# Row differences and sums of the first convolution's bands made on GpSimd during attention

## The chip, the cores and the metric

The kernel runs on one core of a Trainium2 chip. The metric is the device time of one execution in microseconds (us); the median of three executions of the kernel before is 2505.46 us.

## The reference, cut to what matters

The input `x` is 4 images of 128 channels and 64 x 64 pixels in float32. Two layers follow each other:

```python
# layer 0: attention over all 4096 pixels of an image, 4 heads of 32 channels
x_norm = group_norm(x)
q, k, v = split(einsum('oc,bchw->bohw', qkv_w, x_norm) + qkv_b, 3)
attn = softmax(einsum('bhid,bhjd->bhij', q, k) * d ** -0.5)
y0 = x + einsum('oc,bchw->bohw', proj_w, einsum('bhij,bhjd->bhid', attn, v)) + proj_b

# layer 1: two 3x3 convolutions with weights quantized to 3 bits
out = relu(batchnorm(conv3x3(y0, lsq_quantize(w1, alpha1)), gamma1, beta1))
out = batchnorm(conv3x3(out, lsq_quantize(w2, alpha2)), gamma2, beta2)
out = relu(out + y0)
```

`batchnorm` takes its mean and variance over all images and pixels, so no image can leave the first convolution before all have been convolved.

## The kernel before, in words

**Attention.** The work is cut into 32 blocks n (4 images times 8 blocks of 512 queries). A block goes through 32 key tiles kt of 128 keys. For a key tile, `scores` makes the scores of four heads in two halves (L442) and ScalarE exponentiates each half out of PSUM into the SBUF tile `p` (L444). `weights` multiplies `p` with the values into `acc` (L456) and adds `p` to the sum of the exponentials: for most key tiles VectorE adds it to `r` (L469, L471); for the six key tiles in `MOVED` = 4, 9, 14, 19, 24, 28 a DMA issued by GpSimd adds it to `rm` instead (L464 copies the first, L466 accumulates the others, L492 merges `rm` into `r`). Nine tiles `p` exist, so the exponential of key tile kt + 9 waits until the adder of kt is done with its tile. The scores run ahead of the weights by three pairs of matmul groups.

**What lies beside attention.** `schedule(n, before)` returns a list of small tasks for block n, each with the half of a key tile after which it is put out: the end of the block before (its sums, its division, its projection, the residual, the store of y0 to DRAM by a GpSimd DMA at L548), loads of x, projections of the next image, and the quantization of the two convolutions' weights (`quant_tasks`). The quantized weights of the first convolution stay in SBUF in `wq[0]`; those of the second go to DRAM in `wqd` and come back into SBUF during the first convolution.

**The convolutions.** The 4 images are cut into 16 bands m of 16 rows. As a matmul in the full float32 format is not used here, each operand is split into a rounded part `hi` and a rest `lo`. A band goes in one of two ways. Plain (`conv`, L828): 9 taps, two parts, two halves, 36 matmuls of 512 columns. By two (`conv_by_two`, L874): two output rows at a time, from differences of rows two apart (`vo`) and sums and differences of neighbouring rows (`vi`), with mixed weights `wmix` for the inner two terms and the plain weights for the outer two; 24 matmuls. `BY_TWO` names the bands that go by two in each convolution.

For a band by two the mixing is done by VectorE (L595, L597, L598), ScalarE rounds the results to `uo`, `ui` (L600), VectorE makes the rests `lo`, `li` (L604). Behind the matmuls ScalarE copies one result out of PSUM (L884), VectorE adds the inner terms (L887, L888) and the outer ones (L891, L893), and ScalarE squares the result for the variance (L957). `layer` goes over the bands; for band m the order on the engines is: matmuls of m; copy(m); mixing and rounding of m + 2; inner(m); rests of m + 2; `later`; outer(m); square(m). `first` says what `later` is in the first convolution: the load of band m + 3 and, at m = 5, `count_bad`, which ends in a small matmul `nbad` on TensorE (L1004) that counts values over a limit.

Bands 0 and 1 are split while the last attention block still runs; their matmuls and the projection of the last block come first when attention is over, then attention's pools are closed (`att.close()`), the pools `mid` and `upper` are opened in their place, and the bands from 2 on follow. The Tile framework derives the semaphores; within an engine the order is the order of the program.

Of the kernel before, what the change touches and what calls it, by code (L numbers as in the profile page):

```python
# [16 lines left out]
F32 = mybir.dt.float32  # L17
AF = mybir.ActivationFunctionType
ALU = mybir.AluOpType
# [3 lines left out]
P = 128  # L23
GROUP = 16
HEADS = 4
D = 32
TAPS = 9
FB = 512
# [3 lines left out]
ROUND = 1.5 * 2.0**23  # L32


F32R = mybir.dt.float32r
# [43 lines left out]
def _fast_body(ctx, tc, x, norm_w, norm_b, qkv_wt, qkv_b, proj_wt, proj_b,  # L79
               w1, alpha1, gamma1, beta1, w2, alpha2, gamma2, beta2, out, cnt):  # L80
    nc = tc.nc
# [3 lines left out]
    RB = FB // W  # L85
# [50 lines left out]


    dram = ctx.enter_context(tc.tile_pool(name="dram", bufs=1, space=bass.MemoryType.DRAM))
    wq = [const.tile([P, TAPS, P], F32R, name="wq0")]
    wqd = dram.tile([P, TAPS, P], F32, name="wqd")  # L140
    alpha_s = []
    gfac = 1.0 / math.sqrt(float(P * P * TAPS) * QP)

    def quant_tasks(pool):

        tasks = []
        for i, (w, alpha) in enumerate(((w1, alpha1), (w2, alpha2))):
            al = const.tile([P, 1], F32, name=f"al{i}")
            nc.gpsimd.dma_start(out=al, in_=alpha.partition_broadcast(P))
            t = {n: const.tile([P, 1], F32, name=f"{n}{i}")  # L150
                 for n in ("ag", "a_s", "a_c", "a_h", "a_l", "inv", "ninv")}
            alpha_s.append(t["a_s"])


            def scalars(al=al, t=t):
                nc.vector.tensor_scalar(t["ag"], al, gfac, None, ALU.mult)
                nc.vector.tensor_tensor(t["a_s"], al, t["ag"], ALU.subtract)
                nc.vector.tensor_tensor(t["a_s"], t["ag"], t["a_s"], ALU.add)
                nc.vector.tensor_scalar(t["a_c"], t["a_s"], 4097.0, None, ALU.mult)
                nc.vector.tensor_tensor(t["a_h"], t["a_c"], t["a_s"], ALU.subtract)  # L160
                nc.vector.tensor_tensor(t["a_h"], t["a_c"], t["a_h"], ALU.subtract)
                nc.vector.tensor_tensor(t["a_l"], t["a_s"], t["a_h"], ALU.subtract)
                nc.vector.reciprocal(t["inv"], t["a_s"])
                nc.vector.tensor_scalar(t["ninv"], t["inv"], -1.0, None, ALU.mult)
                yield

            tasks.append(scalars)
            for c in range(3):


                def taps(i=i, c=c, w=w, t=t):
# [21 lines left out]
                    if i == 0:  # L193
                        nc.vector.tensor_scalar(wq[0][:, cs, :], q0, ROUND, None, ALU.subtract)
                    else:
                        nc.vector.tensor_scalar(ql, q0, ROUND, None, ALU.subtract)
                        nc.gpsimd.dma_start(out=wqd[:, cs, :], in_=ql)
                    yield

                tasks.append(taps)  # L200
        return tasks

# [3 lines left out]


    kpool = ctx.enter_context(tc.tile_pool(name="kpool", bufs=NB + 1))
    pss = ctx.enter_context(tc.tile_pool(name="pss", bufs=3, space=PSUM))
    psa = ctx.enter_context(tc.tile_pool(name="psa", bufs=2, space=PSUM))  # L210
    y0 = [dram.tile([P, N], F32, name=f"y0_{b}") for b in range(B)]
    BR = 2 * RB
    KW = (BR + 2) * PW
    att = ExitStack()
# [5 lines left out]
    rpool = att.enter_context(tc.tile_pool(name="rpool", bufs=1))  # L220
    sums = att.enter_context(tc.tile_pool(name="sums", bufs=2))
    wpool = att.enter_context(tc.tile_pool(name="wpool", bufs=1))

    def stack_tile(name):
        return kpool.tile([P, KW], F32R, name=name, tag="k")

    def f32(t):
        return t.bitcast(F32)
# [351 lines left out]

    BY_TWO = (set((3, 4, 6, 7, 9, 10, 12, 13, 14)), set((2, 3, 4, 6, 7, 9, 10, 12, 13, 14)))

    def mixed_parts(t, name):

# [34 lines left out]
    def load_band(b, g):  # L621
        raw[b, g] = t = band_tile(f"t0_{b}_{g}")
        inner, lo, hi = border(t, g)
        nc.sync.dma_start(out=inner, in_=y0[b].rearrange("p (h w) -> p h w", w=W)[:, lo:hi, :])

    def split_band(b, g):
        ready[0, b, g] = split(raw[b, g], f"0_{b}_{g}")
# [53 lines left out]
    def schedule(n, before):  # L681
# [8 lines left out]
        def add(kt, f):  # L690
            todo.append((2 * kt + 1, f))
# [79 lines left out]
        if b == B - 1 and qb < NB - 1:  # L771
            for kt in (3, 11, 21):
                add(kt, lambda: next(pieces, None))
        elif 0 < b and qb == 0:
            for kt in (3, 12, 17, 22, 26) + ((29,) if b == 1 else ()):
                add(kt, lambda: next(pieces))
        if n == len(blocks) - 1:
            add(5, lambda: load_band(0, 0))
            add(13, lambda: split_band(0, 0))
            add(17, lambda: load_band(0, 1))  # L780
            add(24, lambda: split_band(0, 1))
            add(27, lambda: load_band(0, 2))
        return sorted(todo, key=lambda t: t[0])

    pieces = (piece for task in quant_tasks(stage) for piece in task())
    steps = len(blocks) * NK
# [46 lines left out]
    def conv_tile(i, b, g):  # L833
        return pss.tile([P, 2, FB], F32, name=f"c{i}_{b}_{g}", tag="s")


    early = [conv_tile(0, *bandlist[m]) for m in range(2)]
# [4 lines left out]
    split_band(*bandlist[2])  # L842
    load_band(*bandlist[3])
# [7 lines left out]

    mid = ctx.enter_context(tc.tile_pool(name="mid", bufs=1))
    cv = [mid.tile([P, N], F32, name=f"cv{b}") for b in range(B)]
    wq.append(mid.tile([P, TAPS, P], F32R, name="wq1"))
    upper = ctx.enter_context(tc.tile_pool(name="upper", bufs=12))
    wmix = mid.tile([P, 2, 3, P], F32R, name="wmix")

    def mix_weights(i):

        g0, g1, g2 = (f32(wq[i])[:, 3 * k : 3 * k + 3, :] for k in range(3))  # L860
        h = f32(stack_tile(f"wsum{i}"))[:, : 3 * P].rearrange("p (t o) -> p t o", o=P)
        nc.vector.tensor_tensor(h, g0, g2, ALU.add)
        nc.vector.tensor_scalar(h, h, 0.5, None, ALU.mult)
        for k, f in enumerate((0.5, -0.5)):
            nc.vector.scalar_tensor_tensor(wmix[:, k, :, :], g1, f, h, ALU.mult, ALU.add)
# [12 lines left out]
    def rows_of_two(a, c, y, sums):  # L878
# [15 lines left out]
                                           accum_out=sums[:, 1:2])  # L894

        return copy, inner, outer

    mix_weights(0)


    a_q, a_g, a_n = ([small.tile([P, 1], F32, name=f"{n}{i}") for i in range(2)]
# [108 lines left out]
    def first(m):  # L1010
        begin = rest = nothing
        if 0 < m and m + 2 < len(bandlist):
            begin, rest = parts_of(0, m + 2, raw[bandlist[m + 2]])

        def later():
            if m == 5:
                count_bad()
                raw["w"] = f32(stack_tile("raw_w"))[:, : TAPS * P].rearrange("p (t o) -> p t o", o=P)
                nc.sync.dma_start(out=raw["w"], in_=wqd)
            if m == 6:  # L1020
                nc.vector.tensor_copy(wq[1], raw["w"])
            if 0 < m < len(bandlist) - 3:
                load_band(*bandlist[m + 3])

        return begin, rest, later

# [24 lines left out]
    relu_band(1)  # L1051
    for f in parts_of(1, 1, raw[1, 1]):
        f()
    mix_weights(1)
    relu_band(2)


# [500 lines left out]
```

## Time and profile before

| | us |
|---|---|
| median of 3 executions (2505.22 to 2505.53) | 2505.46 |
| the profiled execution | 2506.32 |
| its span, from the first to the last instruction | 2504.6 |
| preparation, to | 30 |
| attention, 32 blocks, to | 2234.4 |
| bands 0 and 1 and the last projection, to | 2254.8 |
| first convolution from band 2 on, to | 2360.1 |
| batch norm, second convolution, output, to | 2504.6 |

The mean granted clock of TensorE is 0.994 of full speed. PE stands for TensorE, ACT for ScalarE, DVE for VectorE, POOL for GpSimd, SP for SyncE; L444 is line 444 of the kernel before. A row of the profile's groups reads: line, engine, operation, output<-input by the program's names, shapes, count | busy us, mean ns of one | idle time of the engine before them and what ended it.

### The profile page before, as it was taken

What the parts mean: (1) busy time and instruction counts of PE and PEld (TensorE: products, weight loads), DVE (VectorE), ACT (ScalarE), POOL (GpSimd) and SP (SyncE); (2) the same over time, 40 slices, a digit from 0 to 9 for tenths busy, and PEclk for the clock granted to TensorE, in tenths of its full rate; (3) what the DMA queues carried; (4) which work ended last, traced back from release to release, by engine and by line L of the source; (5) the groups of instructions that cost most, each with busy time, mean ns of one, the idle gap of its engine ahead of it and who ended that gap; (6) DMA issues with size and microseconds to landing.
All of it is one profiled execution on the core that took longest, in us unless ns stands there. A gap on an engine that the chain in (4) does not pass through costs nothing. (4 is left out here: it accounts for less than half of the span.)

```text
span 2504.6 us, 64822 instructions
## 1 busy us (share of the span) xinstructions
PE 2459.0 (98%) x28480; PEld 1462.1 (58%) x28480; DVE 2206.2 (88%) x1552; ACT 2147.0 (86%) x2344; POOL 281.9 (11%) x463
## 2 busy tenths in 40 slices
PE   9999999999999999999999999999999999998995
PEld 6555555555555555555555555555555555566774
DVE  6899888898988888889988898889999999988797
ACT  5999888999988899999988898998999999964475
POOL 2111111111011111110011111110000000100000
PEclk9999999999999999999999999999999999999998
DMA  6777677787767666788767767688656656664205
GB/s 197 189 185 170 163 178 174 171 200 184 181 156 168 178 165 165 160 201 191 167 149 184 167 157 170 170 204 185 147 129 153 142 131 148 154 128 97 86 1 203
DMA packets 148954, 403.84 MB, mean 161 GB/s; under 512 B 59416, under 2 KB 60184, under 8 KB 120120
## 3 DMA queue, kind: packets, MB, share of 16 engines
q0 software_dynamic: 45840, 280.39, 49.0%
q1 hardware_dynamic: 100952, 113.60, 17.2%
q8 instruction: 225, 3.69, 0.6%
q10 hardware_dynamic: 1872, 5.64, 0.6%
q14 instruction: 65, 0.53, 0.1%
HBM read 107.48 MB, written 56.42 MB: 65 GB/s over the span
## 5 line engine op out<-in xcount | busy, mean ns | idle before, releaser
L444 ACT ACTIVATE p<-s 128x1024 f32<-128x1024 f32 x2048 | 1950.5, 1032 | 202.2 <-PE s L442 154.0
L471 DVE TENSOR_TENSOR r<-r,p 128x2048 f32<-128x2048 f32 x768 | 1758.2, 2289 | 65.3 <-ACT p L444 15.0
L442 PE MATMUL s<-q,k 64*128 64x512 f32 x8192 | 1139.7, 409 | 1.9 <-ACT p L444 1.7
L456 PE MATMUL acc<-p,v 128*32 128x256 f32 x16384 | 1026.6, 383 | 0.0
L442 PEld LDWEIGHTS s<-q,k 64*128 64x128 f32 x8192 | 715.7, 185 | 410.9 <-issue 166.1
L456 PEld LDWEIGHTS acc<-p,v 128*32 128x32 f32 x16384 | 462.8, 109 | 483.4 <-issue 248.4
L466 POOL DMA_DIRECT2D rm<-p x160 | 139.1, 869 | 799.4 <-ACT p L444 556.8
L352 DVE SCALAR_TENSOR_TENSOR kst<-pk,b,kst 128x512 fp32r<-128x512 f32 x32 | 24.0, 750 | 83.3 <-PE s L442 68.5
L469 DVE TENSOR_TENSOR r<-p,p 128x2048 f32<-128x2048 f32 x32 | 73.2, 2288 | 12.8 <-ACT p L444 12.8
L352 DVE SCALAR_TENSOR_TENSOR qst<-pq,b,qst 128x512 fp32r<-128x512 f32 x32 | 24.0, 751 | 58.5 <-PE s L442 47.5
L957 ACT ACTIVATE uo<-cv,shift 128x1024 fp32r<-128x1024 f32 x19 | 21.9, 1153 | 53.1 <-DVE cv L893 50.5
L356 POOL DMA_DIRECT2D qd<-qst x31 | 23.6, 761 | 266.7 <-DVE qst L352 225.3
L828 PE MATMUL c<-hi,wq 128*128 128x512 f32 x198 | 51.2, 403 | 1.2 <-ACT hi L1045 1.2
L828 PE MATMUL c<-lo,wq 128*128 128x512 f32 x198 | 50.8, 401 | 0.0
L492 POOL DMA_DIRECT2D r<-rm x31 | 26.2, 844 | 218.2 <-PE s L442 61.8
L970 ACT COPY cv<-c 128x512 f32<-128x512 f32 x22 | 12.9, 586 | 38.4 <-DVE st L969 38.4
L828 PEld LDWEIGHTS c<-hi,wq 128*128 128x128 f32 x198 | 36.9, 188 | 13.1 <-issue 2.1
L828 PEld LDWEIGHTS c<-lo,wq 128*128 128x128 f32 x198 | 37.3, 188 | 10.0
L874 PE MATMUL c<-ui,wmix 128*128 128x512 f32 x114 | 35.2, 418 | 6.8 <-ACT cv L970 4.2
L356 POOL DMA_DIRECT2D kd<-kst x27 | 20.0, 740 | 178.6 <-DVE kst L352 169.9
L351 ACT ACTIVATE kst<-pk,b 128x512 fp32r<-128x512 f32 x32 | 22.3, 699 | 18.1 <-PE pk L317 18.0
L488 PE MATMUL l<-r,ones 128*32 128x256 f32 (+1 forms) x504 | 37.7, 383 | 0.0
(258 smaller groups left out, 1137.1 us busy)
## 6 DMA issues: line engine op xcount, KB each, us to landing
rm<-p POOLq DMA_DIRECT2D x192, 1024.0 KB, 7.8
q<-qd SPq DMA_DIRECT2D x248, 128.0 KB
r<-rm POOLq DMA_DIRECT2D x31, 1024.0 KB, 7.6
x<-in_x_dram SPq DMA_DIRECT2D x86, 256.0 KB
k<-kd SPq DMA_DIRECT2D x124, 128.0 KB
qd<-qst POOLq DMA_DIRECT2D x31, 512.0 KB, 5.6
kd<-kst POOLq DMA_DIRECT2D x27, 512.0 KB, 4.7
y<-x POOLq DMA_DIRECT2D x32, 256.0 KB, 6.1
```

The lines of the kernel that those rows point to most:

```text
L352: nc.vector.scalar_tensor_tensor(lo, ps[what], bias, t[:, 0, :], ALU.add, ALU.subtract)
L356: (nc.sync if start else nc.gpsimd).dma_start(out=dst[b, j].rearrange("s p n -> p s n"), in_=t)
L442: nc.tensor.matmul(s[:, i, :], k[r, half, c0 : c0 + P], q[r, half, part, :], start=(part == 0), stop=(part == 1))
L444: nc.scalar.activation(pts[step][:, 2 * half : 2 * half + 2, :], s, AF.Exp, scale=SCALE)
L456: nc.tensor.matmul(acc[n][h * D : (h + 1) * D, cs], v[:, kt % KB, h * D : (h + 1) * D], pt[:, h, cs], start=(kt == 0 and half == 0), stop= ...
L466: nc.gpsimd.dma_start(out=msum[n], in_=pt, accum_op=ALU.add)
L469: nc.vector.tensor_tensor(rsum[n], pts[step - 1], pt, ALU.add)
L471: nc.vector.tensor_tensor(rsum[n], rsum[n], pt, ALU.add)
L488: nc.tensor.matmul(t["l"][h * D : (h + 1) * D, cs], ones, r[:, h, cs], start=first, stop=end)
L492: nc.gpsimd.dma_start(out=rsum[n], in_=msum[n], accum_op=ALU.add)
L828: nc.tensor.matmul(ps.rearrange("p (r w) -> p r w", w=W), w[:, tap, :], part[:, r0 + kh : r0 + kh + RB, kw : kw + W], start=(n == 0), stop ...
L874: nc.tensor.matmul(ps.rearrange("p (r w) -> p r w", w=W), w[:, kw, :], part[m][:, :, kw : kw + W], start=(n == 0), stop=(n == 5))
```

## The change

During attention blocks 8 to 31 GpSimd makes, from rows of y0 that earlier blocks have stored, the row differences and sums of half a band per block and stores them in DRAM: block n makes half (n - 8) mod 2 of band 2 + (n - 8) // 2. A load of 10 rows of y0 is put out at key tile 17, the difference at key tile 21, the sum and difference of neighbouring rows at key tile 25. In the first convolution bands 2 to 13 all go by two and are loaded from DRAM already mixed; bands 14 and 15 go plain. The quantized weights of both convolutions go to DRAM; those of the first are loaded for bands 0 and 1 into a buffer of attention's sums, and both are loaded into `mid` by ScalarE's DMA queue when attention's pools are closed. `wmix` takes over the buffer of the new tile `ahead` and is made before the first band. The pool of the tiles `p` and `MOVED` are as before.

```diff
-    wq = [const.tile([P, TAPS, P], F32R, name="wq0")]
-    wqd = dram.tile([P, TAPS, P], F32, name="wqd")
+    wqd = [dram.tile([P, TAPS, P], F32, name=f"wqd{i}") for i in range(2)]
...
+    both = keep.tile([P, 10 * W + RB * PW], F32, name="ahead", tag="m")
+    ahead = both[:, : 10 * W].rearrange("p (r w) -> p r w", w=W)
+    mixed = both[:, 10 * W :].rearrange("p (r w) -> p r w", w=PW)
...
-    BY_TWO = (set((3, 4, 6, 7, 9, 10, 12, 13, 14)), set((2, 3, 4, 6, 7, 9, 10, 12, 13, 14)))
+    BY_TWO = (set(range(2, 14)), set((2, 3, 4, 6, 7, 9, 10, 12, 13, 14)))
...
+    def ahead_parts(m, p):
...
+        def load():
...
+            nc.sync.dma_start(out=ahead[:, lo - r0 : hi - r0, :],
+                              in_=y0[b].rearrange("p (h w) -> p h w", w=W)[:, lo:hi, :])
+        def outer():
+            nc.gpsimd.tensor_tensor(mixed[:, :, 1 : 1 + W], ahead[:, 0:RB, :],
+                                    ahead[:, 2 : RB + 2, :], ALU.subtract)
+            nc.gpsimd.dma_start(out=mixes[m][:, 0, p * RB : (p + 1) * RB, :], in_=mixed)
+        def inner():
+            odd, even = ahead[:, 1 : RB + 1 : 2, :], ahead[:, 2 : RB + 2 : 2, :]
+            h = RB // 2
+            nc.gpsimd.tensor_tensor(mixed[:, :h, 1 : 1 + W], odd, even, ALU.add)
+            nc.gpsimd.tensor_tensor(mixed[:, h:, 1 : 1 + W], even, odd, ALU.subtract)
+            for k in range(2):
+                r = k * RB + p * h
+                nc.gpsimd.dma_start(out=mixes[m][:, 1, r : r + h, :], in_=mixed[:, k * h : (k + 1) * h, :])
...
+    def load_mixed(m):
+        raw[m] = [f32(stack_tile(f"{n}{m}"))[:, : BR * PW].rearrange("p (r w) -> p r w", w=PW)
+                  for n in ("vo", "vi")]
+        for k, t in enumerate(raw[m]):
+            nc.sync.dma_start(out=t, in_=mixes[m][:, k, :, :])
...
+    def split_mixed(m, tile):
...
+        def mix():
+            for u, v in zip(hi, (outer, inner)):
+                nc.scalar.copy(u, v)
+        def rest():
+            for u, v, w in zip(hi, (outer, inner), lo):
+                nc.vector.tensor_tensor(w, v, f32(u), ALU.subtract)
...
+        if n >= NB:
+            load, outer, inner = ahead_parts(2 + (n - NB) // 2, (n - NB) % 2)
+            add(17, load)
+            add(21, outer)
+            add(25, inner)
...
-            add(27, lambda: load_band(0, 2))
+            add(26, first_weights)
+            add(30, lambda: load_mixed(2))
...
+    wmix = keep.tile([P, 2, 3, P], F32R, name="wmix", tag="m")
...
+    mix_weights(wq[0], stage.tile([P, 2, FB], F32, name="wsum0", tag="k")[:, 0, : 3 * P])
...
-    wq.append(mid.tile([P, TAPS, P], F32R, name="wq1"))
+    wq = [mid.tile([P, TAPS, P], F32R, name=f"wq{i}") for i in range(2)]
+    for i in range(2):
+        nc.scalar.dma_start(out=f32(wq[i]), in_=wqd[i])
...
         if 0 < m and m + 2 < len(bandlist):
-            begin, rest = parts_of(0, m + 2, raw[bandlist[m + 2]])
+            if m + 2 in BY_TWO[0]:
+                begin, rest = split_mixed(m + 2, lambda n: upper.tile([P, BR, PW], F32R, name=n, tag="u"))
+            else:
+                begin, rest = parts_of(0, m + 2, raw[bandlist[m + 2]])
...
             if m == 5:
                 count_bad()
-                raw["w"] = f32(stack_tile("raw_w"))[:, : TAPS * P].rearrange("p (t o) -> p t o", o=P)
-                nc.sync.dma_start(out=raw["w"], in_=wqd)
-            if m == 6:
-                nc.vector.tensor_copy(wq[1], raw["w"])
             if 0 < m < len(bandlist) - 3:
-                load_band(*bandlist[m + 3])
+                if m + 3 in BY_TWO[0]:
+                    load_mixed(m + 3)
+                else:
+                    load_band(*bandlist[m + 3])
```

More of the change, by code (lines that the diff above doesn't have):

```diff
@@ L192, in taps @@
                     cs = slice(3 * c, 3 * c + 3)
[L193 to L197, printed above, removed]
+                    nc.vector.tensor_scalar(ql, q0, ROUND, None, ALU.subtract)
+                    nc.gpsimd.dma_start(out=wqd[i][:, cs, :], in_=ql)
                     yield
@@ L208, in _fast_body @@
     kpool = ctx.enter_context(tc.tile_pool(name="kpool", bufs=NB + 1))
+    keep = ctx.enter_context(tc.tile_pool(name="keep", bufs=1))
     pss = ctx.enter_context(tc.tile_pool(name="pss", bufs=3, space=PSUM))
@@ L211, in _fast_body @@
     y0 = [dram.tile([P, N], F32, name=f"y0_{b}") for b in range(B)]
+    mixes = {}
     BR = 2 * RB
@@ L222, in _fast_body @@
     wpool = att.enter_context(tc.tile_pool(name="wpool", bufs=1))
+    both = keep.tile([P, 10 * W + RB * PW], F32, name="ahead", tag="m")
+    ahead = both[:, : 10 * W].rearrange("p (r w) -> p r w", w=W)
+    mixed = both[:, 10 * W :].rearrange("p (r w) -> p r w", w=PW)
+    for c in (0, W + 1):
+        nc.gpsimd.memset(mixed[:, :, c : c + 1], 0.0)
     def stack_tile(name):
@@ L624, in load_band @@
         nc.sync.dma_start(out=inner, in_=y0[b].rearrange("p (h w) -> p h w", w=W)[:, lo:hi, :])
+    def ahead_parts(m, p):
+        b, g = bandlist[m]
+        if p == 0:
+            mixes[m] = dram.tile([P, 2, BR, PW], F32, name=f"mix{m}")
+        r0 = g * BR + p * RB - 1
+        lo, hi = max(r0, 0), min(r0 + 10, H)
+        def load():
+            if r0 < 0:
+                nc.gpsimd.memset(ahead[:, 0, :], 0.0)
+            if r0 + 10 > H:
+                nc.gpsimd.memset(ahead[:, 9, :], 0.0)
+            nc.sync.dma_start(out=ahead[:, lo - r0 : hi - r0, :],
[12 more added lines that the diff above has]
+                nc.gpsimd.dma_start(out=mixes[m][:, 1, r : r + h, :], in_=mixed[:, k * h : (k + 1) * h, :])
+        return load, outer, inner
+    def load_mixed(m):
[4 more added lines that the diff above has]
+    def split_mixed(m, tile):
+        outer, inner = raw[m]
+        hi, lo = ([tile(f"{n}{k}0_{m}") for k in "oi"] for n in "ul")
+        ready[(0, *bandlist[m])] = [
+            (o[:, 0::2, :], i[:, : BR // 2, :], i[:, BR // 2 :, :], o[:, 1::2, :], o)
+            for o, i in (hi, lo)]
+        def mix():
[4 more added lines that the diff above has]
+                nc.vector.tensor_tensor(w, v, f32(u), ALU.subtract)
+        return mix, rest
     def split_band(b, g):
@@ L781, in schedule, with first_weights @@
             add(24, lambda: split_band(0, 1))
-            add(27, lambda: load_band(0, 2))
+            add(26, first_weights)
+            add(30, lambda: load_mixed(2))
         return sorted(todo, key=lambda t: t[0])
+    wq = []
+    def first_weights():
+        t = sums.tile([P, HEADS, FB], F32, name="wq_early", tag="r").rearrange("p h n -> p (h n)")
+        t = t[:, : TAPS * P].bitcast(F32R).rearrange("p (t o) -> p t o", o=P)
+        nc.sync.dma_start(out=f32(t), in_=wqd[0])
+        wq.append(t)
     pieces = (piece for task in quant_tasks(stage) for piece in task())
@@ L834, in conv_tile, with mix_weights @@
         return pss.tile([P, 2, FB], F32, name=f"c{i}_{b}_{g}", tag="s")
+    wmix = keep.tile([P, 2, 3, P], F32R, name="wmix", tag="m")
+    def mix_weights(w, h):
+        g0, g1, g2 = (f32(w)[:, 3 * k : 3 * k + 3, :] for k in range(3))
+        h = h.rearrange("p (t o) -> p t o", o=P)
+        nc.vector.tensor_tensor(h, g0, g2, ALU.add)
+        nc.vector.tensor_scalar(h, h, 0.5, None, ALU.mult)
+        for k, f in enumerate((0.5, -0.5)):
+            nc.vector.scalar_tensor_tensor(wmix[:, k, :, :], g1, f, h, ALU.mult, ALU.add)
+    mix_weights(wq[0], stage.tile([P, 2, FB], F32, name="wsum0", tag="k")[:, 0, : 3 * P])
     early = [conv_tile(0, *bandlist[m]) for m in range(2)]
@@ L841, in _fast_body @@
     conv(ready[0, 0, 0], early[0][:, 1, :], 1, wq[0])
-    split_band(*bandlist[2])
-    load_band(*bandlist[3])
+    for f in split_mixed(2, lambda n: stack_tile(n)[:, : BR * PW].rearrange("p (r w) -> p r w", w=PW)):
+        f()
+    load_mixed(3)
     last["sums_at_once"]()
@@ L853, in _fast_body @@
     cv = [mid.tile([P, N], F32, name=f"cv{b}") for b in range(B)]
-    wq.append(mid.tile([P, TAPS, P], F32R, name="wq1"))
+    wq = [mid.tile([P, TAPS, P], F32R, name=f"wq{i}") for i in range(2)]
+    for i in range(2):
+        nc.scalar.dma_start(out=f32(wq[i]), in_=wqd[i])
     upper = ctx.enter_context(tc.tile_pool(name="upper", bufs=12))
[L856 to L865, printed above, removed]
     def conv_by_two(parts, a, c, i):
@@ L896, in rows_of_two @@
         return copy, inner, outer
-    mix_weights(0)
     a_q, a_g, a_n = ([small.tile([P, 1], F32, name=f"{n}{i}") for i in range(2)]
@@ L1053, in _fast_body @@
         f()
-    mix_weights(1)
+    mix_weights(wq[1], f32(stack_tile("wsum1"))[:, : 3 * P])
     relu_band(2)
```

## The prediction

> **What bounds the kernel now.** I read the page's first list, then the windows view cut into stages, then the waits of attention, the timeline of the first convolution's start, and last its groups of instructions by form. The page's busy times:
>
> ```profile
> PE 2459.0 (98%) x28480; PEld 1462.1 (58%) x28480; DVE 2206.2 (88%) x1552; ACT 2147.0 (86%) x2344; POOL 281.9 (11%) x463
> ```
>
> The windows view (busy us and instructions of PE, PEld, DVE, ACT, POOL; then clock, DMA share, GB/s):
>
> ```profile
> 560.00:1100.00 540.00, 538.71 (x6670) 309.06 (x6668) 480.28 (x296) 488.00 (x530) 65.64 (x87) 1.00 0.72 171
> 1660.00:2234.40 574.40, 572.91 (x6873) 324.51 (x6871) 534.06 (x328) 531.10 (x568) 58.52 (x84) 1.00 0.69 153
> 2254.80:2276.90 22.10, 15.42 (x65) 10.97 (x61) 18.64 (x34) 7.86 (x11) 1.47 (x13) 0.97 0.41 91
> 2275.50:2282.30 6.80, 5.40 (x13) 4.25 (x14) 5.60 (x9) 3.04 (x4) 0.00 (x0) 0.50 0.18 32
> 2282.40:2360.10 77.70, 77.70 (x326) 60.85 (x326) 63.61 (x105) 35.71 (x50) 1.68 (x20) 1.00 0.44 118
> ```
>
> Attention (to 2234.4) is PE's: busy all the time, with DVE at 89 to 93%. In the first convolution PE is the bound from 2282.4 to its end at 2360.1; before that it stood still twice and ran once at half clock (third and fourth row). The change touches both stages: it takes work out of the convolution and puts it beside attention.
>
> The waits in attention (us in total, times, longest) from 560 to 2230:
>
> ```profile
> POOL rm L466 <- ACT p L444: 473.7, 65, 11.3
> POOL rm L466 <- DMA rm<-p: 180.2, 26, 11.7
> ACT p L444 <- PE s L442: 112.3, 307, 2.3
> ACT p L444 <- DMA rm<-p: 4.0, 5, 1.3
> PE s L442 <- ACT p L444: 1.3, 6, 0.3
> ```
>
> POOL mostly waits, so it has time. But 26 of its accumulating DMAs wait for the one before them to land (1 MB, 7.8 us), and five times an exponential waited for such a landing: that chain is nearly full.
>
> **Attention, what is added.** For 24 blocks (n from 8 to 31): an SP load of 320 KB at key tile 17, one POOL difference 128x512 with a 264 KB store, two POOL operations 128x256 with two 132 KB stores; in all 72 POOL operations, 72 POOL DMAs, 24 loads.
>
> POOL's own time: a DMA issue there takes 0.57 to 0.87 us (L464, L466, L548). No row has a POOL operation on two tensors of this size. Lower bound: the same form on DVE, 0.69 us for 128x512, so some 1.4 us for the three. Upper bound, an estimate: POOL's 128x1 power at L132 takes 0.56 us where memsets of one column take 0.10; five times the DVE row would be 7 us a block. Block lengths are 62.6 to 74.6 us, POOL is busy 5.5 to 10.9 us of them; it fits in either case. I take 2 to 3 us a block, nearer to the DVE row, the one of the same form.
>
> What it is moved past: POOL's order is accumulate(19), difference, store, accumulate(24), two operations, two stores, accumulate(28). Each accumulate waits for the exponential of its key tile, some 8 to 10 us after the last, so the operations behind the one before are through by then. What they do delay is data: 264 KB at the rate of the accumulates (1 MB in 7.8 us) is 2.0 us of transfer between 19 and 24 and again between 24 and 28. From the landings in the trace and the start of the exponential nine key tiles later, which takes that buffer, I have the time to spare: block 15 has 0.1 us at 24 and 0.3 at 28; block 23 has 1.2 and 0.4; block 8 has 1.3 at 28; block 11 has 1.8 at 24; block 17 has 2.6 at 28; nearly all others 3 to 7. With 2.0 us more each, ACT loses about 1.9 + 1.6 + 0.7 + 0.2 = 4.4 us, and as the scores lead by three pairs PE feels perhaps half, 2 us. The load and the rest of the traffic (0.85 MB on some 10.8 MB a block) make other landings later too; I add 1 us.
>
> DVE: if a POOL operation holds DVE up for its own length, a block loses 2 to 3 us of DVE. DVE's idle time in a block is 2.2 us at n=9 and 17, 3.0 to 5.3 at 8, 16 and 24 to 31, and 7 to 12.6 elsewhere, and an add can come 2 to 4 us late before an exponential misses its buffer. So this costs 0.5 us or so. Attention in all: +3.5 us, from 0 (all hidden) to +10.
>
> The Trainium skill's GPSIMD Engine Reference (its measured table of `tensor_tensor`) has an add of 2048 elements at 4497 ns on GpSimd and 2293 on VectorE; the trace's L471 has 2289 for the latter, and no run here shows the former. By it the three operations would take an estimated 2.5 us a block.
>
> **First convolution, what is removed.** The rows from 2280 to 2355:
>
> ```profile
> L957 ACT ACTIVATE uo<-cv,shift 128x1024 fp32r<-128x1024 f32 x9 | 10.4, 1153 | 30.1 <-DVE cv L893 30.1
> L604 DVE TENSOR_TENSOR li<-vi,ui 128x1056 fp32r<-128x1056 f32 x7 | 8.8, 1255 | 0.0
> L604 DVE TENSOR_TENSOR lo<-vo,uo 128x1056 fp32r<-128x1056 f32 x7 | 8.8, 1253 | 0.0
> L595 DVE TENSOR_TENSOR vo<-t 128x1056 f32<-128x1056 f32 x7 | 8.8, 1252 | 0.0
> L888 DVE TENSOR_TENSOR cv<-c,cv 128x512 f32<-128x512 f32 x8 | 5.5, 692 | 0.3
> L598 DVE TENSOR_TENSOR vi<-t 128x528 f32<-128x528 f32 x7 | 4.9, 702 | 0.0
> L884 ACT COPY cv<-c 128x512 f32<-128x512 f32 x8 | 4.6, 574 | 0.7 <-PE c L874 0.7
> ```
>
> DVE loses the mixing of nine bands, 1.25 + 0.70 + 0.70 = 2.65 us each, 24 us. As PE is the bound, that alone gives nothing. What counts is that three more bands go by two: 24 matmuls in place of 36, at 0.24 us (three in 0.72 in the timeline): 3 x 12 x 0.24 = 8.6 us less of PE.
>
> The early stalls, from the timeline of PE:
>
> ```profile
> 2266.27 0.98 PE L874 MATMUL c<-ui,wmix 128*128 128x512 f32 x3 [2.62 <-ACT ui L600]
> 2267.57 0.99 PE L874 MATMUL c<-li,wmix 128*128 128x512 f32 x3 [0.31 <-DVE li L604]
> 2276.90 1.65 PE L874 MATMUL c<-ui,wmix 128*128 128x512 f32 x3 [3.61 <-ACT cv L970]
> ```
>
> They come from DVE mixing band 3 and 4 while it also has the last residual and statistics. With the mixing gone they should go: 2.62 + 0.31 + 3.61 = 6.5 us, and the half clock after the second (0.50 over 6.8 us, twelve matmuls that take 0.43 in place of 0.24) 2.3 us. In all 8.8.
>
> **What is late next.** Three things, of which two are new waits.
>
> First, the weights. Band 2 now goes by two, and half of its matmuls use `wq[0]`, which is fetched anew after attention's pools close. The order of the changed kernel shows that fetch waiting on the last store of y0, as its place is freed then. That store landed at 2258.3 (POOL's memset at L934 waited for it until 2258.67). No row loads 576 KB on ACT's queue: bounds are 3.0 us (the store of a third of the second weights, 192 KB) and 4.4 (1 MB in 7.8 us). PE reaches the point at 2257.7 (2254.8 and twelve matmuls) and idles until 2261.5 to 2263.5 with the issue: 4 to 6 us. I take 5.5, by the row of the larger transfer.
>
> Second, the count of large values. Its matmul stands after band 5 on PE and needs `bad`, which stands after the split of band 7 on DVE. In before this cost nothing, as PE was behind. Now a by-two band on DVE and ACT is a loop: copy 0.57, inner sums 0.69 + 0.69, splits 1.25 + 1.25, outer sums 0.69 + 0.69, square 1.15 + 0.19 = 7.2 us, or 6.7 by the distance of starts in the trace (L604's two start at 2265.1 and 2266.3), longer than PE's 5.8 (24 x 0.24). Counted from wq0 at 2262.5, band 2's outer sums end at 2267, those of band 4 at 2281, and the split of band 7 and `bad` at 2288 to 2291. PE would be through with band 5 at 2254.8 + 5.5 + 4 x 5.77 = 2283.4: idle of 5 to 8 us, I take 7, and 1 us for the half clock that followed the 3.61 us idle above.
>
> Third, the loop itself: from band 8 on PE is at about the loop's place; at 6.7 us it costs PE nothing, at 7.2 PE waits up to another 4 us by band 13. I take 1.
>
> Sum for the convolution: -8.6 - 8.8 + 5.5 + 7 + 1 + 1 = -2.9 us; from -10 (both waits half hidden) to +2. The band whose plain matmuls replace a by-two band (14) is in the 3 x 12.
>
> The `wmix` sums move ahead of the first matmuls, and the copy of the other weights (0.76 us of DVE) goes: nothing, beside other work. The second convolution and the tail are the same instructions: nothing.
>
> **Sum.** The profiled run took 2506.32 us (span 2504.6 and 1.7 around it), 0.86 above the median of 2505.46. 2506.32 - 2.9 + 3.5 = 2506.9; less 0.86 is 2506.1, say 2506.0: the two parts cancel. Its own range is 2500.5 to 2510.5, and 0.2% (5.0 us) is about what a measurement of this kernel can tell from no change.
>
> **Rivals.** (1) Faster: the two waits cost little, because wq0 lands by 2259 or `bad` is ready early. Then -8.6 - 8.8 + 2 + 3 + 1 = -11.4, with attention at 0 to 2 some 2495. For it: PE did lose 8.8 us to DVE's mixing, and DVE is freed of 24 us. Against: both waits stand in the order.
>
> (2) Slower: POOL's operations stop DVE for a long time each. The nearest row speaks both ways: a POOL memset of 128x18 took 1.05 us where DVE's cast ran, and 0.16 in the middle of an add:
>
> ```profile
> 2220.63 1.05 POOL L560 MEMSET t<- 128x18 f32 x1
> 2220.85 0.77 DVE L573 CAST hi<-t 128x1188 fp32r<-128x1188 f32 x1
> 2231.03 4.68 DVE L471 TENSOR_TENSOR r<-r,p 128x2048 f32<-128x2048 f32 x2
> 2231.97 0.16 POOL L560 MEMSET t<- 128x18 f32 x1
> ```
>
> If each of three operations costs DVE 1.75 us (5.25 a block), blocks 8, 9, 16, 17 and 24 to 31 lack 18 us beyond their idle time; the 2 to 4 us that an add may be late come off once in each of three runs of blocks: +9. At a full add each (2.29, 6.9 a block) it is 38 - 9 = +29. It decides from about 1.4 us an operation, where the run from 24 to 31 goes short. With the full chain of accumulates and -2.9, 2513 to 2531; I price it at 2515. For it: DVE's 93% in the last quarter. Against: 2 to 3 us a block is all that I expect POOL to need.
>
> The skill's SBUF — State Buffer (on the shared port pair) says that a VectorE instruction with two SBUF inputs and a GpSimd instruction that reads SBUF exclude each other for a whole instruction. L471 is such a one; no row here shows such a pair. By the estimate above DVE would lose 2.5 us a block, which leaves case 2 at +1.
>
> **Numbers.** Forecast 0.40, rival 1 0.25, rival 2 0.33, 0.02 for others. The range takes most of both: 2494 to 2520.
>
> **What would show it.** Right: PE idle of some 5 us in band 2 with ACT's weights DMA as releaser, another after band 5 at `nbad`, the convolution's end 3 us earlier counted from attention's end, attention 3 us longer with ACT waiting for rm<-p. Wrong: no idle at either point (rival 1); L471's mean well above 2289 ns and PE waiting for ACT in blocks 24 to 31 (rival 2).

## Result: 13 us slower, all of it and a little more lost in attention

The changed kernel took 2518.39 us (median of 5 executions, 2517.38 to 2519.24) against 2505.22 us of the kernel before on the same chip: a ratio of 1.0053, 95% interval 1.0039 to 1.0068. The profiled execution took 2518.83 us, its span 2517.1.

| stretch, us | before | after | difference |
|---|---|---|---|
| attention's end (the copy of the last block's `acc`) | 2234.5 | 2248.2 | +13.7 |
| of it blocks 8 to 31 | 1638.9 | 1653.8 | +14.9 |
| from there to the first matmul of the second convolution | 129.3 | 128.0 | -1.3 |
| from there to the end of the span | 140.8 | 141.0 | +0.2 |

The stretches are read from one profiled execution of each kernel and cut at the same instructions in both traces. The predicted 2506.0 was too low by 12 us, inside the stated range, and the loss came in the term that had been given 3.5 us.

The page's busy times after, to be held against those before:

```profile
PE 2455.6 (98%) x28444; PEld 1456.2 (58%) x28444; DVE 2231.9 (89%) x1538; ACT 2151.5 (85%) x2351; POOL 453.3 (18%) x588
```

DVE was meant to lose the 24 us of mixing and has 26 us more. The groups view says where (busy us, mean ns; line numbers are from here on those of the kernel whose trace is read, so L475 is the add that was L471):

```profile
L475 DVE TENSOR_TENSOR r<-r,p 128x2048 f32<-128x2048 f32 x768 | 1786.6, 2326 | 58.2 <-ACT p L448 7.2
L647 POOL TENSOR_TENSOR ahead<-ahead 128x512 f32<-128x512 f32 x24 | 49.1, 2046 | 50.7 <-DMA ahead<-y 50.7
L655 POOL TENSOR_TENSOR ahead<-ahead 128x256 f32<-128x256 f32 x24 | 48.2, 2009 | 0.0
L654 POOL TENSOR_TENSOR ahead<-ahead 128x256 f32<-128x256 f32 x24 | 39.0, 1626 | 17.6 <-DMA mix<-ahead 17.4
```

The same adds had a mean of 2289 ns before. Their 88 that overlap a POOL operation have 2615 ns, the other 488 of blocks 8 to 31 2289. The view of the tile `ahead` gives the shortest, median and longest of POOL's three operations:

```profile
L647 POOL TENSOR_TENSOR ahead<-ahead x24: 1279/1984/2737, 644.4 to 2223.2; 128x512 f32<-128x512 f32 x24
L654 POOL TENSOR_TENSOR ahead<-ahead x24: 724/1436/2831, 651.6 to 2235.4; 128x256 f32<-128x256 f32 x24
L655 POOL TENSOR_TENSOR ahead<-ahead x24: 719/2772/2891, 652.4 to 2236.9; 128x256 f32<-128x256 f32 x24
```

At best the half-size operation takes 0.72 us; its median in the second place is 2.77, longer by 2.05, which is about one add of 2.29. By these lengths each engine waits for the other.

The waits of attention show who suffers. Of TensorE's waits for DVE there were two in the kernel before (560 to 2230):

```profile
PE po L317 <- DVE av L537: 1.1, 1, 1.1
PE gw L291 <- DVE b L286: 0.9, 1, 0.9
```

In the changed kernel (560 to 2240):

```profile
POOL rm L470 <- ACT p L448: 401.8, 69, 11.7
ACT p L448 <- PE s L446: 123.6, 309, 3.3
POOL rm L470 <- DMA rm<-p: 86.7, 16, 8.2
POOL ahead L647 <- DMA ahead<-y: 50.7, 11, 11.9
PE po L321 <- DVE av L541: 8.8, 8, 2.0
ACT p L448 <- DMA rm<-p: 5.4, 4, 1.7
PE gv L267 <- DVE mean L263: 2.3, 1, 2.3
PE gw L295 <- DVE b L290: 1.5, 2, 1.1
```

The chain of accumulating DMAs, the main suspect of the forecast, has not become worse: ACT waited 5.4 us for it after 4.0, POOL 86.7 after 180.2. In the starts of the matmuls nine projections (blocks 9, 10, 11, 15, 17, 18, 19, 23 and 31) come late by 0.7 to 2.2 us each beyond the usual step, 10.8 in all; one of them was late before, by 1.2. The group norm of the next image (`gv`, `gw`) comes later by 3.0 us in all in blocks 9, 10 and 18, and one score by 1.4: with the 9.6 us more at the projections 14.0 of the 14.9.

How such a wait arises is seen in the timeline of block 17:

```profile
1274.88 3.19 DVE L475 TENSOR_TENSOR r<-r,p 128x2048 f32<-128x2048 f32 x1
1278.83 0.16 DVE L272 TENSOR_TENSOR ga<-gr,nw 128x1 f32<-128x1 f32 x1 [0.69 <-POOL gr L132]
1279.03 2.05 DVE L274 SCALAR_TENSOR_TENSOR gc<-mean,ga,nb 128x1 f32<-128x1 f32 x1
1279.38 1.00 POOL L654 TENSOR_TENSOR ahead<-ahead 128x256 f32<-128x256 f32 x1
1280.08 0.98 POOL L655 TENSOR_TENSOR ahead<-ahead 128x256 f32<-128x256 f32 x1
1281.57 0.68 DVE L541 TENSOR_TENSOR av<-av,rc 128x512 f32<-128x512 f32 x1
```

A DVE instruction of one column (`gc`) took 2.05 us, and it ended with POOL's two sums. The same instruction in the same block before:

```profile
1270.06 0.22 DVE L270 SCALAR_TENSOR_TENSOR gc<-mean,ga,nb 128x1 f32<-128x1 f32 x1
```

Together with the 0.9 us on the add, `av` is 2.7 us late, and TensorE, which had been waiting for it since 1280.1, starts the projection at 1282.3 (2.43 us after the matmul before it).

In the convolution the two new waits stand where they were predicted (timeline of PE):

```profile
2270.76 0.87 PE L951 MATMUL c<-li,wmix 128*128 128x512 f32 x3
2279.09 1.62 PE L951 MATMUL c_2x<-uo,wq 128*128 128x512 f32 x3 [7.46 <-DMA wq<-wqd]
2280.50 1.48 PE L951 MATMUL c_2x<-lo,wq 128*128 128x512 f32 x3
2306.18 0.19 PE L1079 MATMUL nbad<-ones,bad 128*1 128x1 f32 x2 [4.21 <-DVE bad L1077]
2306.30 1.65 PE L951 MATMUL c<-ui,wmix 128*128 128x512 f32 x3
```

Behind each, three matmuls take some 1.3 us from start to start in place of 0.72, for 13 matmuls, and the windows view has the granted clock at 0.50 from 2279.1 to 2284.3 and from 2306.3 to 2311.6.

### The profile page after: what moved, and what is told of

It reads as the page before. It is cut to its first block, busy times and chain, and to the rows that moved or that the text cites. A ratio compares the mean times of both kernels' runs of the same rounds, so it can differ in the third digit from the quotient of the medians.

```text
span 2517.1 us, 64973 instructions
## 1 busy us (share of the span) xinstructions
PE 2455.6 (98%) x28444; PEld 1456.2 (58%) x28444; DVE 2231.9 (89%) x1538; ACT 2151.5 (85%) x2351; POOL 453.3 (18%) x588
## 4 chain that ended last, share of the span: by engine, by line
PE 80%; DVE 7%; issue 6%; DMA 4%; ACT 3%; POOL 1%; SPq 0%; ACTq 0%; POOLq 0%; DVEq 0%
PE s L446 37%; PE acc L460 33%; DVE r L475 3%; DMA rm<-p 2%; ACT p L448 2%; PE c L951 1%; PE po L321 1%; PE pk L321 1%; PE l L492 1%; PE pq L321 1%; PE pv L321 1%; PE c L901 1%; DMA rc<-rd 1%; PE idle L314 0%; ACT res L1173 0%
## 5 line engine op out<-in xcount | busy, mean ns | idle before, releaser
L475 DVE TENSOR_TENSOR r<-r,p 128x2048 f32<-128x2048 f32 x768 | 1786.6, 2326 | 58.2 <-ACT p L448 7.2
L470 POOL DMA_DIRECT2D rm<-p x160 | 140.9, 881 | 627.1 <-ACT p L448 497.9
L647 POOL TENSOR_TENSOR ahead<-ahead 128x512 f32<-128x512 f32 x24 | 49.1, 2046 | 50.7 <-DMA ahead<-y 50.7
L468 POOL DMA_DIRECT2D rm<-p x32 | 17.9, 558 | 172.0 <-ACT p L448 97.7
L655 POOL TENSOR_TENSOR ahead<-ahead 128x256 f32<-128x256 f32 x24 | 48.2, 2009 | 0.0
L321 PE MATMUL po<-av,wp 128*32 128x512 f32 x256 | 33.7, 598 | 10.0 <-DVE av L541 9.9
L964 DVE TENSOR_TENSOR cv<-cv,c 128x512 f32<-128x512 f32 x22 | 15.1, 686 | 31.9 <-ACT cv L961 31.9
L654 POOL TENSOR_TENSOR ahead<-ahead 128x256 f32<-128x256 f32 x24 | 39.0, 1626 | 17.6 <-DMA mix<-ahead 17.4
L951 PE MATMUL c<-ui,wmix 128*128 128x512 f32 x132 | 40.6, 417 | 0.7 <-ACT cv L1045 0.7
L951 PE MATMUL c<-li,wmix 128*128 128x512 f32 x132 | 40.0, 413 | 0.1
## 6 DMA issues: line engine op xcount, KB each, us to landing
q<-qd SPq DMA_DIRECT2D x248, 128.0 KB
k<-kd SPq DMA_DIRECT2D x124, 128.0 KB
```

What stands on the lines that cost most here:

```text
L321: nc.tensor.matmul(out[cs, :], w[:, cs], x, start=True, stop=True)
L470: nc.gpsimd.dma_start(out=msum[n], in_=pt, accum_op=ALU.add)
L475: nc.vector.tensor_tensor(rsum[n], rsum[n], pt, ALU.add)
L647: nc.gpsimd.tensor_tensor(mixed[:, :, 1 : 1 + W], ahead[:, 0:RB, :], ahead[:, 2 : RB + 2, :], ALU.subtract)
L655: nc.gpsimd.tensor_tensor(mixed[:, h:, 1 : 1 + W], even, odd, ALU.subtract)
L951: nc.tensor.matmul(ps.rearrange("p (r w) -> p r w", w=W), w[:, kw, :], part[m][:, :, kw : kw + W], start=(n == 0), stop=(n == 5))
```

## Experiments

All times are medians, and each ratio is to the kernel before on the same chip. "Attention's end" and "the convolution's stretch" are those of the table above, from one profiled execution of each kernel. Where attention is the same, its end differs by up to 2 us between such executions: 2234.5 and 2232.5 with the old attention, 2248.2, 2248.6 and 2247.7 with the changed one. The stretch is 127.5 to 128.2 in all eight kernels that leave the changed convolution as it is.

**1. What in attention costs: arithmetic, occupancy or traffic.**

```diff
-            nc.gpsimd.tensor_tensor(mixed[...], ...)        # without the operations: all three left out
+            for _ in range(4):                              # with memsets: 4, 5 and 6 in their places
+                nc.gpsimd.memset(mixed[...], 0.0)
```

Without the operations:

> Leaves out the three GpSimd operations per block (the stores carry zeros, so the first convolution gets wrong sums); loads, stores and all else stay. Attention ended at 2248.2 us in the changed kernel and at 2234.5 before. Theory A (GpSimd operations that read SBUF stop VectorE, the division av comes late and TensorE waits for it at the projection): attention ends at 2235 to 2238, the time is 2505 to 2508. Theory B (the 0.85 MB per block and the GpSimd DMAs make the accumulating DMAs late): it ends at 2245 or later, 2515 or more.

Measured: 2504.89 us, ratio 0.9995 (0.9986 to 1.0005); attention's end 2233.2, 2 us before the earliest that theory A gave.

With memsets:

> Puts memsets of the same output (4, 5 and 6 of them, some 2 us, 1.5 us and 1.9 us) in the place of the three GpSimd operations, so that GpSimd is busy for about as long but reads nothing (the mixed rows are zeros). Theory A with reading as the cause: as without the operations, attention ends at 2235 to 2238. If it is GpSimd's time in its queue that counts (theory C: the accumulates and the group norm's power wait behind it), it stays above 2244.

Measured: 2504.25 us, ratio 0.9996 (0.9986 to 1.0005); attention's end 2232.9. POOL was as busy as with the operations. The windows view of blocks 8 to 31 (PE, PEld, DVE, ACT, POOL), first of the changed kernel, then without the operations, then with memsets:

```profile
594.30:2248.20 1653.90, 1638.12 (x20029) 932.84 (x20026) 1526.24 (x906) 1494.60 (x1614) 361.30 (x403) 1.00 0.73 176
```

```profile
594.10:2233.20 1639.10, 1634.83 (x20029) 934.72 (x20026) 1484.13 (x905) 1494.51 (x1613) 230.76 (x331) 1.00 0.73 178
```

```profile
594.70:2232.90 1638.20, 1634.29 (x20027) 934.30 (x20025) 1484.03 (x905) 1494.70 (x1613) 362.07 (x691) 1.00 0.73 178
```

Blocks 8 to 31 took 1638.9 us before. The DMA traffic is the same in all three and costs nothing that can be seen. POOL's busy time is the same in the first and third, and costs nothing either. DVE's busy time is 42 us longer where POOL reads SBUF, and only there: 1.75 us a block, 0.58 us an operation.

**2. Is it the wait for the load.** The memsets also did away with POOL's wait for the ten rows, so this was tried apart:

```diff
-            add(17, load)
+            add(8, load)
```

> The load of the ten rows of y0 is put out at key tile 8 in place of 17; all else is as in the changed kernel, where GpSimd waited 51 us in 11 blocks for that load (up to 11.9) with an accumulate and once the group norm's power behind it. If these waits are what costs: attention ends some 8 us or more earlier than 2248, below 2241. Theory A (the reading operations stop VectorE): GpSimd's wait goes, attention's end stays within 3 us of 2248.

Measured: 2522.98 us, ratio 1.0079 (1.0062 to 1.0096); attention's end 2252.2. The wait for the load was gone, and attention ended 4 us later rather than earlier; 4 is a little over the 3 that theory A allowed, and what made it later was not looked for. The wait for the load is not the cause.

**3. Does one input do less harm.**

```diff
-            nc.gpsimd.tensor_tensor(mixed[:, :h, 1 : 1 + W], odd, even, ALU.add)
+            nc.gpsimd.tensor_copy(mixed[:, :h, 1 : 1 + W], odd)
```

(and the other two alike, the difference as two copies)

> The three operations on two tensors are replaced by four copies from the same rows (two of 128x512 and two of 128x256, one SBUF input each; the mixed rows are then wrong). Theory A with any reading as the cause: VectorE's adds are again longer beside them, and attention ends above 2241. If only operations with two inputs shut VectorE out: 2233 to 2236, as with memsets.

Measured: 2507.72 us, ratio 1.0017 (1.0007 to 1.0026); attention's end 2234.4. A miss for both: the 103 adds beside the copies are longer (2390 ns), so one input is enough to hold DVE up, yet attention's end is only 1.2 us later than without the operations. The copies hold it for less (0.62 us at the shortest for 128x512, 0.39 for 128x256, against 1.28 and 0.72), and DVE loses 15 us in blocks 8 to 31 in place of 42, 0.63 a block:

```profile
594.80:2234.40 1639.60, 1635.27 (x20027) 933.50 (x20026) 1499.21 (x905) 1494.56 (x1613) 383.14 (x427) 1.00 0.73 178
```

But the profiled execution is the fastest of the ten (2504.36), and the median is 3.4 us above it. By the ratios the copies cost some 5.5 us against the kernel without the operations, where the three operations cost 14.5: a third of the time for a third of DVE's loss. So this run does not show that anything but the size of the loss counts; where the slower executions lost their time is open.

**4. Which date.** A date is here a point in TensorE's own order at which it takes a result from DVE. First the projection three halves of a key tile later:

```diff
-            at_half(ends[18], before["project"])
-            at_half(ends[18] + 2, before["store"])
+            at_half(ends[19], before["project"])
+            at_half(ends[19] + 2, before["store"])
```

> Only the projection and the store of a block are put out three halves of a key tile later (about 3 us); GpSimd's work stays. Theory A: av is 0.7 to 2.2 us late, so the nine waits at the projection vanish, 9.6 us: attention ends at 2237 to 2240, the time is 2507 to 2511; the waits at the group norm of blocks 9, 10 and 18 (about 3 us) stay. Theory B, if the accumulates hold back TensorE: no change.

Measured: 2516.71 us, ratio 1.0045 (1.0028 to 1.0061); attention's end 2243.8, a gain of 4.4 us where 8 to 11 were expected; the ratio's interval overlaps that of the changed kernel, so only the trace shows the gain. TensorE no longer waits at the projection, but DVE now empties the projection's PSUM tile too late for the next block's `acc` (waits view, 590 to 2245):

```profile
PE acc L460 <- DVE x L551: 5.8, 5, 2.3
PE gv L267 <- DVE mean L263: 2.4, 1, 2.4
PE gw L295 <- DVE b L290: 2.0, 1, 2.0
```

Then POOL's operations behind the projection:

```diff
-            add(21, outer)
-            add(25, inner)
+            add(21 if n == len(blocks) - 1 else 28, outer)
+            add(25 if n == len(blocks) - 1 else 30, inner)
```

> Only the place changes: the difference goes to key tile 28 and the sums to key tile 30 (the last block keeps 21 and 25), behind the projection. Theory A: VectorE loses the same time, but where only the tiles p wait for it, so TensorE's waits at the projection go, about 9 us: attention ends at 2238 to 2241, the time is 2508 to 2511. Theory B: no change, within 2 us of 2248. Theory C: a gain of a few us at most.

Measured: 2529.88 us, ratio 1.0101 (1.0081 to 1.0122); attention's end 2254.1: the expectation failed. The waits of 590 to 2255 tell why:

```profile
POOL ahead L654 <- DMA mix<-ahead: 114.3, 23, 6.7
DVE av L541 <- DMA rc<-rd: 10.7, 3, 5.1
PE po L321 <- DVE av L541: 8.3, 5, 3.3
PE l L492 <- DMA r<-rm: 6.0, 5, 2.8
```

The sums write into the tile that the difference's store is still reading, and POOL stands 5 us a block for it, with the merge of the sums of exponentials behind it in its queue; TensorE then waits for that merge. What follows from the sums is late too: in three blocks `av` waits for the reciprocals `rc` to land, and the projections with it. This was a new chain of waits, and it hid what was to be tested. The next version has the difference at key tile 30 and the sums at key tile 2 of the following block, behind the merge:

```diff
+            for f in left:
+                add(2, f)
+            left.clear()
...
+                add(30, outer)
+                left.append(inner)
```

> As the run that moved GpSimd's operations behind the projection, but without its fault (there the sums waited 114 us in all, 4.8 a block, for the difference's store to land, and the merge of the sums waited behind them): the difference stands at key tile 30 and the two sums at key tile 2 of the next block, behind the merge. Theory A (what costs is a late VectorE where TensorE has a date with it: projection, group norm): the waits at the projection go, attention ends at 2236 to 2241 in place of 2248.2, the time is 2506 to 2511. If VectorE's lost time itself costs (1.75 us a block), attention stays above 2246 wherever the operations stand.

Measured: 2510.17 us, ratio 1.0018 (1.0009 to 1.0028); attention's end 2239.8, 8.4 us earlier. DVE's total is the same as in the changed kernel (2231.6 us against 2231.9), so the same time was lost at another place. Of the late projections two are left (1.7 us in block 23, which was late before, and 0.9 in the last block, which keeps the old places); the group norm's waits have grown (waits of 594 to 2250):

```profile
PE gw L295 <- DVE b L290: 3.7, 2, 3.2
PE gv L267 <- DVE mean L263: 2.5, 2, 1.7
PE po L321 <- DVE av L541: 2.4, 2, 1.6
```

By the starts of the matmuls the group norm is later by 5.5 us than in the kernel before, after 3.0 in the changed one. With the projections' 1.5 that makes up the 7.0 us that blocks 8 to 31 still take longer than before. So the same loss of DVE costs half as much at another place, and what it still costs stands at the next date: lost DVE time counts where TensorE has a date with DVE.

**5. The convolution.** Both new waits mended:

```diff
+    wlow = ctx.enter_context(tc.tile_pool(name="wlow", bufs=1))
+    wq = [wlow.tile([P, TAPS, P], F32R, name=f"wq{i}") for i in range(2)]
     mid = ctx.enter_context(tc.tile_pool(name="mid", bufs=1))
     cv = [mid.tile([P, N], F32, name=f"cv{b}") for b in range(B)]
-    wq = [mid.tile([P, TAPS, P], F32R, name=f"wq{i}") for i in range(2)]
```

(and `big` and `bad` of `count_bad` made ahead of the convolution)

> Two edits for the two new waits in the first convolution: the weights' pool is opened ahead of the large pool, so that their fetch waits for value tiles and not for the last store of y0; and the reduction and comparison behind the count of large values are made ahead of the convolution. In the changed kernel the waits are 7.5 and 4.2 us, each followed by matmuls at half clock (about 2.2 us each). From attention's end to the first matmul of the second convolution it took 127.9 us. If only the waits count: 112 to 114. If the loop of VectorE and ScalarE (6.7 to 7.2 us a band against 5.8 of TensorE) is late next: 120 to 125.

Measured: 2515.69 us, ratio 1.0041 (1.0026 to 1.0055); the stretch is 124.4 us, a gain of 3.6. The wait for the weights is gone (the fetch is issued at 2259.3 in place of 2272.4). At `nbad` 2.1 us are left, now as a wait for VectorE's outer sums (`cv`, L969), and then the loop shows (timeline of PE):

```profile
2326.68 0.98 PE L952 MATMUL c<-li,wmix 128*128 128x512 f32 x3 [0.72 <-DVE li L681]
2333.48 0.99 PE L952 MATMUL c<-li,wmix 128*128 128x512 f32 x3 [0.79 <-DVE li L681]
2340.30 0.98 PE L952 MATMUL c<-li,wmix 128*128 128x512 f32 x3 [0.79 <-DVE li L681]
2347.10 0.98 PE L952 MATMUL c<-li,wmix 128*128 128x512 f32 x3 [0.82 <-DVE li L681]
```

One band each 6.8 us, with 24 matmuls of 0.24 in it, 5.8. The loop is cut by putting the square behind the next band's copy and roundings:

```diff
                 copy()
                 begin()
+                while waiting:
+                    waiting.pop()()
                 inner()
...
+                def square(y=y, k=k, m=m):
+                    junk = stack_tile(f"junk{m}")[:, : 2 * FB]
+                    nc.scalar.activation(junk, y, AF.Square, bias=shift[:, 1:2], accum_out=squares[:, k : k + 1])
+                waiting.append(square)
```

> The run with both waits mended, and ScalarE's square of a band put behind the copy and the roundings of the band after it (it writes its unused output to a tile of its own), so that the loop from VectorE's outer sums over the square to the next copy is cut; VectorE then needs 4.9 us a band and ScalarE 4.1. If the loop is late next: the stretch falls to 110 to 114 us. If VectorE or the loads are: no gain over the run before it.

Measured: 2506.31 us, ratio 1.0004 (0.9995 to 1.0014); the stretch is 115.5 us, 8.9 less than with the waits mended alone and 12.5 less than in the changed kernel; the upper end of what was expected, 114, was missed by 1.5. From band 4 on TensorE stands still nowhere for more than 0.3 us; waits of 2.5 us for `ui` and 0.5 for `li` of band 3 are left. The loop was the third bound: to cut it was worth 8.9 us, the 2.1 us left at `nbad` and the slow matmuls behind them included, where mending the two waits alone was worth 3.6.

Does that edit owe anything to the change? In the kernel before:

> The kernel before with one of the three edits of the first convolution: ScalarE's square of a by-two band behind the copy and the roundings of the next by-two band, with a tile of its own. There TensorE was the bound from 2282.4 us on, and the early waits come from VectorE's mixing. If the faster combined kernel owes its gain to the moved arithmetic (three bands fewer go plain and VectorE's loop shrinks to 4.9 us): no change here, within 2 us of 2505. If the edit alone brings it: 2497 or less.

Measured: 2503.99 us, ratio 0.9997 (0.9987 to 1.0006); the stretch is 129.2 us against 129.3. By itself it is worth nothing.

**6. Together.**

> Both: the later place of GpSimd's operations, and the three edits of the first convolution. If the gains add up: attention ends at 2236 to 2241 and the convolution takes 110 to 114, in all 2489 to 2497, less than the kernel before. If the place does not matter: 2500 to 2505.

Measured: 2498.76 us, ratio 0.9974 (0.9964 to 0.9985); attention's end 2238.1, the stretch 116.5. The gains add up to within 2 us, but the time and the stretch lie above what was expected, 2497 and 114.

```diff
-                add(2, f)
+                add(6 if n in (10, 18) else 2, f)
```

> The combined kernel, but in blocks 10 and 18 the two sums left over from the block before stand at key tile 6 in place of 2, as there the group norm of the next image is on its way through VectorE (TensorE waited 2.5 and 3.4 us for it in the combined kernel). If VectorE's lateness at that date is the cause: attention ends 4 to 5 us earlier, at 2233 to 2235, and the time is 2493 to 2496. If the group norm is late anyway (it waited 1.3 us in block 10 before the change too): no more than 1 us.

Measured: 2495.01 us, ratio 0.9965 (0.9954 to 0.9977), faster than the kernel before and the changed one. Attention's end is 2236.6, a gain of 1.5 us there where 4 to 5 were expected: the time lies in its range, but not by that working, and neither 1.5 us nor the two ratios, whose intervals overlap, set this kernel apart from the combined one. The waits of 594 to 2250, first of the combined kernel, then of this one:

```profile
PE gw L295 <- DVE b L290: 5.1, 2, 3.0
```

```profile
PE gw L295 <- DVE b L290: 3.0, 2, 1.7
```

The wait at the group norm is shorter, so the place of those sums may have been part of its cause; one execution of each does not show more. The rest of the lateness (DVE has 2.2 us of idle time in blocks 9 and 17) was not taken apart further.

## Why the prediction was right, and where its steps were not

- **The range held, the forecast's own case did not.** 2518.4 lies in 2494 to 2520 but outside 2500.5 to 2510.5. That it held is owed to the width of the range, which took in both rivals, and in part to luck: 1.6 us more would have left it. No case described what happened. The slower rival's price (2515) was the nearest, though not by its working: it needed 1.75 us lost per operation, and 0.58 was measured; its sign, TensorE waiting for ACT in blocks 24 to 31, did not show (0.5 us from 1660 on). Its bounds of 2513 and 2531 also lie 18 us apart where its terms, +9 and +29, lie 20 apart. Of the forecast's signs, the two waits in the convolution came, the 3 us of ACT waiting for `rm<-p` did not.
- **The step that failed** is the one on DVE: "So this costs 0.5 us or so." The loss it started from, 2 to 3 us a block, was near the 1.75 measured. The cover was wrong: it was tested against DVE's idle time in a block and the nine tiles `p`, and both hold. The step left out what TensorE takes from DVE in its own order: `av` for the projection, `mean` and `b` for the group norm, the emptying of the PSUM tile. The sums were put at key tile 25, where `weigh` and with it `av` stands too, so DVE came late just ahead of its date. In place of 0.5 us this cost 14.9. Experiment 1 shows that DVE's loss is the cause, and experiment 4 that its place decides what it costs.
- **The DMA terms** (2 us for the accumulates, 1 for the traffic) measured nothing: the kernel without the operations has all the DMAs, and its blocks 8 to 31 take 1639.1 us after 1638.9.
- **POOL's time** was 5.7 us a block, within the bounds of 1.4 to 7 but twice what was taken. At their shortest the three need 1.28 + 0.72 + 0.72 = 2.7, as taken; the rest is, by the lengths above, waiting for DVE, which the rows of DVE's own operations could not show.
- **The convolution** came out at -1.3 us where -2.9 was said. The weights' wait was 7.5 rather than 5.5 (the fetch was issued at 2272.4, 3.9 us after band 2 had begun, and landed 6.7 later, not 3.0 to 4.4) with its own half clock of some 2 us, which the sum had left out. `nbad` waited 4.2 rather than 7, with more half clock than the 1 that was given. With 2.3 for each half clock, as the forecast took it from the trace before, the sum is -8.6 - 8.8 + 7.5 + 2.3 + 4.2 + 2.3 = -1.1, close to the measured -1.3. The loop, given 1 us, was hidden behind the two waits; it showed once they were gone.
- **The skill's rules.** The estimate from the GPSIMD Engine Reference, 2.5 us a block, agrees with the 2.7 of the shortest operations. SBUF — State Buffer (on the shared port pair) says that a VectorE instruction with two SBUF inputs and a GpSimd instruction exclude each other if the latter reads SBUF, and not if it only writes: 42 us of DVE for the operations, none for the memsets, agrees. The forecast priced that rule as a sum over the idle time, +1 us, and the traces say +14.9.

## What to carry to other kernels

Work moved to an idle engine is not free if it takes time from the engine that it was to relieve; look for each date at which the bounding engine takes something from the slowed one in its own order, and place the moved work right behind such a date, not ahead of it; then look at the next date, as the group norm took up part of what the projections had gained. Average idle time in a block and the depth of a buffer say nothing about those dates. When a wait is mended and little is gained, cut the next loop before giving the change up: here three edits of the convolution and another place in attention took the ratio to the kernel before from 1.0053 to 0.9974.

## What the hardware showed

- A GpSimd operation on two SBUF tensors of 128x512 in float32 took 1.28 us at its shortest, with no VectorE instruction beside it, and one of 128x256 0.72; beside VectorE's adds they took up to 2.9 us. One-column VectorE instructions beside such operations ended with them: 0.22 us became 2.05 beside two, 0.16 became 0.69 beside one.
- GpSimd memsets of some 2 us in a row beside the same adds lengthened none of them (2289 ns with and without).
- After waits of 4.2 and 7.5 us TensorE ran 13 matmuls at about half speed; after one of 2.1 us, and after 2.5 and 0.5 us close together, 6 to 8; in the kernel before, after 2.62 and 0.31 us, none.
